# GNN and expert layer, one core: the routing of the FFN done in two halves, x and result rows by GpSimd's queue

## The chip, the cores and the metric

The kernel runs on one core of a Trainium2 chip. The metric is the device time of one execution in microseconds (us). Engines: PE is TensorE (matmuls; PEld its weight loads), DVE is VectorE, ACT is ScalarE, POOL is GpSimd, SP is SyncE, which here only issues DMAs. Each engine works through its own queue in order; an instruction that waits holds back all that is queued behind it.

## The reference, cut to what matters

There are 10,000 rows of 512 numbers, and 5,000 edges. All of it is 32-bit.

```
x = x + gnn(layernorm(x), edges)     # edge messages, two matmuls, two batch norms, silu
x = x + ffn(layernorm(x))

ffn, for each group of 16 tokens, 64 columns (16 experts x 4 sets), 32 features each:
  logits = x @ controller + tie                       # per token and column
  perm   = (logits == max of logits over the 16)      # one token for each column
  inner  = relu(the chosen token @ f1[:, column, :])  # 32 features
  result[token] = sum over columns of perm * (inner @ f2[column])
```

The change touches the FFN alone, and the last part of the GNN that runs with it: silu(scale * h2 + shift), added to x (the residual), and the layernorm of the sum.

## The kernel before, in words

The GNN ends with h2 stored in HBM by features (`h2s`). The FFN takes the 10,000 rows in ten chunks of 1024 tokens (the last has 784). A chunk has two groups `g` of 512 tokens; a group has four tiles `j` of 128; a pair `q` is two tiles, so a buffer of rows (`x2`, 512 KB) is named by `(q, g)`. The FFN of one chunk goes through these parts:

- `load_y`, `load_x`: h2 by features (four DMAs of 256 KB for each half of the chunk) and x by rows come in.
- `silu` (ACT), then `residual(j)`: PE transposes four blocks of h2 to rows in a PSUM tile `ps` (L544), DVE adds them to x (L545) and takes statistics (L546, L547). `norm(j)`: POOL works out scale and shift (L556 to L559) and writes the normalized rows `xl` (L563).
- `flip(k, q)`: PE transposes `xl` for 128 features `k` (L574), ACT copies that to `xlt` (L578). `logits`: PE multiplies by the controller (L592). `choose(q)`: DVE finds the maximum and `perm` (L608 to L611). `by_token(q)`: PE transposes `perm` (L619), DVE spreads it to `bd` (L624).
- `gather(k, g)`: PE multiplies `xl` by `bd` (L642, 32 matmuls in two PSUM tiles `pb`), so that the chosen tokens stand by column; ACT copies each tile out in two copies (L647).
- `inner(k, e)`: 64 matmuls with half of the f1 weights of features `k` (L664). After the last, ACT takes the relu (L669). Each call takes one block of weights and orders a fetch of another (`f_sb`, L477, 512 KB, five buffers).
- `outer(u, g)`: 64 matmuls with f2 (L686) into two `pb` tiles. They are copied to `it` by ACT (L696), for u of 2 and 3 one of the two by DVE (L694).
- `turn(g, u)`: DVE transposes `it` in blocks (L705). `split(q)`: POOL makes `pv` out of `perm` (L714). `scatter(q, g)`: 64 matmuls give each token its result (L735), DVE adds that to the rows (L739), and they are stored (L740).

The parts of three chunks run in one `step(a, b, e)`: chunk `b` is gathered and goes through both layers, chunk `a` after it gets its residual and its routing, and chunk `e` before it gets its results scattered. There are twelve steps; the first has only an `a`, the last only an `e`. The order of instructions on each engine is that of the calls in `step`, since nearly all are pinned (`pin` keeps the program's order).

In the order of `step` before, the gather stage holds b's gathers and inner layer with e's turns and scatters between them. All of a's residuals stand from the end of that stage into the outer stage, and all of a's flips and logits stand among b's outer calls. The logits use the PSUM tile `pi` of the inner layer. [...]

All DMAs of the FFN are issued by SP, in this order within a step: loads of a's first half of h2 and of two x buffers, the weight fetches, and, between them, each store of e followed by one load of x for a. The row buffers are 10 in turn.

## Time and profile before the change

| | us |
|---|---|
| median of 3 runs (2075.49 to 2083.97) | 2081.48 |
| the profiled execution | 2089.11 |
| its span, first to last instruction | 2087.3 |
| GNN, up to the last of its matmuls | about 1245 |
| from there to the first gather | 38.5 |
| a step of the FFN, mean of the eight from 1357.8 to 1967.0 | 76.2 |
| the last gather to the end | 120 |

The page shows one profiled execution. Busy time is given for each engine, and in the row of slices a digit is a fortieth of the span: PEclk is the clock that TensorE was granted, in tenths of full speed. A group of instructions is named by line, engine and tile (`pb<-f_sb,ib` writes pb and reads f_sb and ib). What stands in brackets or behind an arrow is what ended the wait. "issue" means that the engine waited for nothing that the profile shows.

### The profile page before, as it was taken

Reading aid. Unit: us, or ns where it says so; the run is one execution under the profiler, and the core shown is the slowest. Engines: PE = TensorE matmul, PEld = TensorE weight load, DVE = VectorE, ACT = ScalarE, POOL = GpSimd, SP = SyncE. Lnnn points to the kernel's source line nnn. Section 1 sums busy time; section 2 is a strip of 40 time slices with the busy share of each in tenths; the row PEclk is TensorE's granted clock in tenths of the full one; section 3 lists DMA queues with packets and bytes.
Section 4 is the critical chain, followed back from the end, with each engine's and each line's share of the span. In section 5 each row is a group of like instructions: output and inputs, shape, how many; then the busy total and the mean of one; then the engine's idle time right before and its main releaser. Section 6 shows DMA issues by size and latency. Waiting matters only on the chain. (4 is left out here: it accounts for less than half of the span.)

```text
span 2087.3 us, 44115 instructions
## 1 busy us (share of the span) xinstructions
PE 1821.4 (87%) x19122; PEld 998.7 (48%) x19122; DVE 1152.6 (55%) x1838; ACT 751.2 (36%) x1161; POOL 650.2 (31%) x710
## 2 busy tenths in 40 slices
PE   4885499999999989999999988888888888888765
PEld 2332244444444434444444435566566557556452
DVE  5743367777777673343344433365645645645645
ACT  1332233333333343222223113556555555455331
POOL 7144433333333233223332302412421431431410
PEclk8897699999999999999999995899889997898875
DMA  9977443444444112323233114455665564574331
GB/s 353 360 170 89 112 181 157 159 166 165 162 157 158 59 79 118 138 118 138 118 140 161 57 73 176 163 194 186 211 217 188 174 236 141 187 243 162 112 119 62
DMA packets 125720, 331.89 MB, mean 159 GB/s; under 512 B 10183, under 2 KB 10773, under 8 KB 125462
## 3 DMA queue, kind: packets, MB, share of 16 engines
q1 hardware_dynamic: 116566, 308.09, 40.5%
q0 software_dynamic: 8960, 20.98, 5.0%
q8 instruction: 151, 2.47, 0.5%
q14 instruction: 43, 0.35, 0.1%
HBM read 218.97 MB, written 110.07 MB: 158 GB/s over the span
## 5 line engine op out<-in xcount | busy, mean ns | idle before, releaser
L134 PE MATMUL x<-h_s,w_u 128*128 128x500 f32 x640 | 288.8, 584 | 0.9 <-ACT s L139 0.6
L647 ACT COPY gs<-pb 128x512 f32<-128x512 f32 x304 | 165.3, 631 | 138.9 <-PE pb L642 113.7
L642 PE MATMUL pb<-bd,xl 32*128 32x128 f32 x2504 | 183.2, 334 | 32.7 <-ACT gs L647 24.2
L134 PEld LDWEIGHTS x<-h_s,w_u 128*128 128x128 f32 x640 | 121.9, 191 | 149.3 <-issue 142.9
L696 ACT COPY it<-pb 128x1024 f32<-128x1024 f32 x120 | 120.8, 1044 | 192.4 <-PE pb L686 192.4
L642 PEld LDWEIGHTS pb<-bd,xl 32*128 32x128 f32 x2504 | 163.1, 231 | 50.2 <-ACT gs L647 28.3
L705 DVE STREAM_TRANSPOSE it<-it 128x1024 f32<-128x1024 f32 x160 | 182.4, 1207 | 0.0
L686 PE MATMUL pb<-f_sb,ib 32*32 32x256 f32 x5120 | 153.1, 411 | 27.6 <-ACT it L696 18.4
L556 POOL TENSOR_SCALAR ln_rs<-ln_mv 128x2 f32<-128x2 f32 (+2 forms) x41 | 9.1, 222 | 485.7 <-DVE ln_mv L547 472.1
L134 PE MATMUL z<-h_s,w 128*128 128x500 f32 x320 | 148.5, 587 | 3.3 <-POOL h_s L124 3.3
L144 DVE SCALAR_TENSOR_TENSOR t<-w,s 128x500 f32<-128x500 f32 x60 | 40.7, 678 | 189.3 <-PE w L134 185.9
L134 PE MATMUL z<-h_s,w_u 128*128 128x500 f32 x320 | 143.9, 582 | 0.0
L739 DVE TENSOR_TENSOR x<-pb,x 128x1024 f32<-128x1024 f32 (+1 forms) x40 | 48.1, 1204 | 159.3 <-PE pb L735 159.3
L664 PE MATMUL pi<-gs,f_sb 128*32 128x64 f32 x5120 | 110.6, 248 | 25.1 <-issue 15.9
L714 POOL TENSOR_TENSOR pv<-perm,odd_t 64x512 f32<-64x512 f32 x80 | 102.5, 1281 | 67.5 <-issue 62.5
L124 POOL TENSOR_TENSOR h_s<-hc 128x500 f32<-128x500 f32 x60 | 76.6, 1311 | 148.6 <-PE z L134 148.6
L686 PEld LDWEIGHTS pb<-f_sb,ib 32*32 32x32 f32 x5120 | 72.8, 106 | 94.0 <-ACT it L696 46.7
L735 PE MATMUL pb<-it,pv 64*32 64x256 f32 x2504 | 96.7, 435 | 22.8 <-DVE it L705 14.5
L664 PEld LDWEIGHTS pi<-gs,f_sb 128*32 128x32 f32 x5120 | 94.3, 128 | 41.7 <-issue 24.4
L139 ACT COPY s<-z 128x500 f32<-128x500 f32 x60 | 34.6, 576 | 219.4 <-PE z L134 150.8
L694 DVE COPY it<-pb 128x1024 f32<-128x1024 f32 x40 | 48.9, 1223 | 113.9 <-PE pb L686 113.3
L342 ACT ACTIVATE xt<-xt,ln_sh,ln_rs 125x512 f32<-125x512 f32 x80 | 59.6, 805 | 109.4 <-POOL ln_sh L337 109.4
(176 smaller groups left out, 3119.3 us busy)
## 6 DMA issues: line engine op xcount, KB each, us to landing
f_sb<-in_L_ffn_f_dram SPq DMA_DIRECT2D x160, 512.0 KB
h1s<-h SPq DMA_DIRECT2D x36, 1000.0 KB
agg<-zero SPq DMA_DIRECT2D x10, 2048.0 KB
xt<-in_x_dram SPq DMA_DIRECT2D x20, 1000.0 KB
at<-agg SPq DMA_DIRECT2D x20, 1000.0 KB
hc<-h1s SPq DMA_DIRECT2D x20, 1000.0 KB
h2s<-h SPq DMA_DIRECT2D x20, 1000.0 KB
x<-in_x_dram SPq DMA_DIRECT2D x39, 512.0 KB
```

Source lines behind the costliest of these rows:

```text
L124: eng.tensor_tensor(t[:, k0:k1], q(*x0, k0, k1), q(*x1, k0, k1), op)
L134: nc.tensor.matmul(bank, lhsT=us[n][:, k, m * P:(m + 1) * P], rhs=bs[n][k], start=start and k == 0, stop=k == kb - 1, skip_group_check=True)
L342: nc.scalar.activation(r, r, AF.Identity, bias=self.sh[:RT, j, :], scale=self.rs[:RT, j, :])
L642: pin(nc.tensor.matmul(pg[i][:, r % 2, j], lhsT=self.xl[g, j][s, k * P:(k + 1) * P], rhs=self.bd[s, g, j], start=True, stop=True))
L647: pin(nc.scalar.copy(to[:, 8 * i:8 * i + 8], pg[i][:, :, :, 32 * e:32 * e + 32, :].rearrange("d r j e v -> d (r j) e v")))
L664: pin(nc.tensor.matmul(self.pi[32 * q:32 * q + 32, m, :], lhsT=w[:, F * j:F * (j + 1)], rhs=gs[e][:, c, :], start=(k == 0 and m % 8 == 0), ...
L686: pin(nc.tensor.matmul(po[q // 2][o:o + 32, q % 2, t, :], lhsT=self.ib[s, 8 * e + 2 * u + t, 32 * g:32 * g + 32], rhs=self.w[e][s, t, HD * ...
L694: pin(nc.vector.tensor_copy(dst, src))
L696: pin(nc.scalar.copy(dst, src))
L705: pin(nc.vector.transpose(it, it))
L714: pin(nc.gpsimd.tensor_tensor(pv[dh * ES:(dh + 1) * ES, :, g].rearrange("c v (i t) -> c v i t", t=2 * T), self.perm[s, q].rearrange("c (i ...
L735: pin(nc.tensor.matmul(pr[32 * r:32 * r + 32, dh, i, :], lhsT=pv[s, v, g, tok], rhs=self.it[s, g, :, 2 * (4 * r + 2 * q + i) + v, :], star ...
```

## The change: what it does

- `load_y` and `silu` go by pairs `q` instead of groups `g`: half `q` of both groups in one tile, so that the first half serves tiles 0 and 1 of both groups. The first half of the next chunk is loaded in the outer stage, and its silu is done at the very end of the step before. Pieces of a DMA are 1 KB instead of 2 KB.
- `residual(j, g)` is called for one group at a time. Tiles 0 and 1 are done between the gathers; the flips and logits of the first half stand between the last gathers and inner calls; tiles 2 and 3 follow at the end of the gather stage, with `choose(0)`. Among the outer calls there remain `by_token(0)`, the flips and logits of the second half, `choose(1)` and `by_token(1)`.
- `ps` has one bank instead of two; the bank that this frees holds the logits (`pl`).
- The turns of e are dealt out in smaller lots among the gathers; `split(1)` is made later.
- x comes in by POOL's queue (but for the first chunk), and the results leave by it. Row buffers come from a list of free ones: `scatter` puts its own back, and `load_x` takes the one that has been free the longest.

```diff
-    ps_s = ctx.enter_context(tc.tile_pool(name="ps_s", bufs=2, space=PSUM))
+    ps_s = ctx.enter_context(tc.tile_pool(name="ps_s", bufs=1, space=PSUM))
+    ps_l = ctx.enter_context(tc.tile_pool(name="ps_l", bufs=1, space=PSUM))
...
+    slots = list(range(10))
...
-                n = (4 * self.c + 2 * g + q) % 10
-                x2 = self.x2[q, g] = pf.tile([P, 2, H], F32, name="x2", bufs=8) if n > 1 else pre_x[n]
+                n = self.slot[q, g] = slots.pop(0)
+                x2 = self.x2[q, g] = pf.tile([P, 2, H], F32, name=f"x2_{n}") if n > 1 else pre_x[n]
...
-                nc.sync.dma_start(out=x2[:real, :k, :], in_=self.rows(x, g, o, real, k))
+                to, src = x2[:real, :k, :], self.rows(x, g, o, real, k)
+                if self.c:
+                    pin(nc.gpsimd.dma_start(out=to, in_=src))
+                else:
+                    nc.sync.dma_start(out=to, in_=src)
...
-                pi = ps_i.tile([P, MF, G], F32, name="pi")
-                self.pl = pi.rearrange("p (q m) g -> p q (m g)", q=2)
+                self.pl = ps_l.tile([P, 2, QC], F32, name="pl")
...
-            nc.sync.dma_start(out=self.rows(out, g, o, real, k), in_=self.x2[q, g][:real, :k, :])
+            pin(nc.gpsimd.dma_start(out=self.rows(out, g, o, real, k), in_=self.x2[q, g][:real, :k, :]))
+            slots.append(self.slot[q, g])
```

The order of a step afterwards (`put` calls a part if there is such a chunk; `late` is a, but for the first chunk; `nxt` is the chunk after a; `fl` is flip, `lo` logits):

```
put(e, split, 0); gat(0, 0); turns(0, 0, 2); gat(0, 1)
put(a, residual, 0, 0); turns(0, 2, 4); gat(1, 0)
put(a, residual, 0, 1); put(a, norm, 0); inn(0, 0); turns(0, 4, 5); gat(1, 1)
put(a, residual, 1, 0); inn(0, 1); gat(2, 0)
put(a, residual, 1, 1); put(a, norm, 1); inn(1, 0); turns(0, 5, 8)
put(e, split, 1); gat(2, 1); inn(1, 1); turns(1, 0, 4); gat(3, 0)
fl(0, 0); inn(2, 0); put(late, load_y, 1)
put(e, scatter, 0, 0); put(late, load_x, 1, 0); turns(1, 4, 8); gat(3, 1)
fl(1, 0); lo(0, 0); inn(2, 1); put(a, silu, 1)
put(e, scatter, 1, 0); put(late, load_x, 1, 1); inn(3, 0)
fl(2, 0); lo(1, 0); inn(3, 1); fl(3, 0); lo(2, 0)
put(e, scatter, 0, 1); lo(3, 0)
put(a, residual, 2, 0); put(a, residual, 2, 1); put(a, norm, 2)
put(e, scatter, 1, 1)
put(a, residual, 3, 0); put(a, residual, 3, 1); put(a, norm, 3); put(a, choose, 0)
put(b, outer, 0, 0); put(nxt, load_x, 0, 0); put(nxt, load_x, 0, 1); put(nxt, load_y, 0)
put(b, outer, 0, 1); put(a, by_token, 0); put(b, outer, 1, 0); put(b, outer, 1, 1)
fl(0, 1); put(b, outer, 2, 0); fl(1, 1); lo(0, 1); put(b, outer, 2, 1)
fl(2, 1); lo(1, 1); put(b, outer, 3, 0); fl(3, 1); lo(2, 1); lo(3, 1)
put(a, choose, 1); put(b, outer, 3, 1); put(a, by_token, 1); put(nxt, silu, 0)
```

More of the change, by code (lines that the diff above doesn't have):

```diff
@@ L492, in __init__ @@
             self.tiles = [[(o, min(P, -(-(n - o) // 32) * 32), min(P, n - o)) for o in range(0, n, P)] for n in self.ns]
-            self.x2, self.st, self.mv, self.rs, self.sh, self.yt, self.xl = {}, {}, {}, {}, {}, {}, {}
+            self.x2, self.slot, self.st, self.mv, self.yt, self.xl, self.pv = {}, {}, {}, {}, {}, {}, {}
         def there(self, j):
@@ L504, in row_tile, with load_y @@
             return self.x2[j // 2, g][:, j % 2, :]
-        def load_y(self, g):
-            n = self.ns[g]
-            if g:
+        def load_y(self, q):
+            if q:
                 gs = pf.tile([P, ES // 2, G], F32, name="gs", bufs=4).rearrange("p c g -> p (c g)")
             for k in range(KH):
-                yt = gs[:, k * HC:(k + 1) * HC] if g else pre_y[k]
-                nc.sync.dma_start(out=yt[:, :n], in_=h2s[:, k, self.t0 + g * HC:self.t0 + g * HC + n])
-                if n < HC:
-                    pin(nc.vector.memset(yt[:, n:-(-n // 32) * 32], 0.0))
-                self.yt[g, k] = yt
+                yt = (gs[:, k * HC:(k + 1) * HC] if q else pre_y[k]).rearrange("p (g n) -> p g n", g=2)
+                src = h2s[:, k, self.t0:self.t0 + self.n]
+                if self.full:
+                    nc.sync.dma_start(out=yt, in_=src.rearrange("p (g q n) -> q p g n", g=2, q=2)[q])
+                else:
+                    for g in range(2):
+                        n = min(self.ns[g] - q * QC, QC)
+                        if n > 0:
+                            o = g * HC + q * QC
+                            nc.sync.dma_start(out=yt[:, g, :n], in_=src[:, o:o + n])
+                            if n % 32:
+                                pin(nc.vector.memset(yt[:, g, n:-(-n // 32) * 32], 0.0))
+                self.yt[q, k] = yt
         def rows(self, hbm, g, o, real, k):
@@ L524, in load_x, with silu, residual @@
                 o, m, real, k = self.pair(q, g)
-                n = (4 * self.c + 2 * g + q) % 10
-                x2 = self.x2[q, g] = pf.tile([P, 2, H], F32, name="x2", bufs=8) if n > 1 else pre_x[n]
+                n = self.slot[q, g] = slots.pop(0)
+                x2 = self.x2[q, g] = pf.tile([P, 2, H], F32, name=f"x2_{n}") if n > 1 else pre_x[n]
                 if real < m:
                     pin(nc.vector.memset(x2[:m, 0, :], 0.0))
-                nc.sync.dma_start(out=x2[:real, :k, :], in_=self.rows(x, g, o, real, k))
-        def silu(self, g):
-            for k in range(KH):
-                y = self.yt[g, k][:, :self.ns[g]]
-                pin(nc.scalar.activation(y, y, AF.Silu, bias=sh2[:, k:k + 1], scale=sc2[:, k:k + 1]))
-        def residual(self, j):
-            self.st[j] = pf.tile([P, 2, 6], F32, name="ln_st", bufs=2)
-            self.mv[j] = pf.tile([P, 2, 2], F32, name="ln_mv", bufs=2)
-            for g in self.there(j):
-                o, m, _ = self.tiles[g][j]
+                to, src = x2[:real, :k, :], self.rows(x, g, o, real, k)
+                if self.c:
+                    pin(nc.gpsimd.dma_start(out=to, in_=src))
+                else:
+                    nc.sync.dma_start(out=to, in_=src)
+        def silu(self, q):
+            for k in range(KH):
+                yt = self.yt[q, k]
+                ns = [min(n - q * QC, QC) for n in self.ns]
+                for y in [yt] if ns == [QC, QC] else [yt[:, g, :n] for g, n in enumerate(ns) if n > 0]:
+                    pin(nc.scalar.activation(y, y, AF.Silu, bias=sh2[:, k:k + 1], scale=sc2[:, k:k + 1]))
+        def residual(self, j, g):
+            if g == 0:
+                self.st[j] = pf.tile([P, 2, 6], F32, name="ln_st", bufs=2)
+                self.mv[j] = pf.tile([P, 2, 2], F32, name="ln_mv", bufs=2)
+            if g in self.there(j):
+                _, m, _ = self.tiles[g][j]
                 x2 = self.row_tile(g, j)[:m, :]
@@ L543, in residual @@
                 for k in range(KH):
-                    pin(nc.tensor.transpose(py[:m, k * P:(k + 1) * P], self.yt[g, k][:, o:o + m], ident))
+                    o = (j % 2) * P
+                    pin(nc.tensor.transpose(py[:m, k * P:(k + 1) * P], self.yt[j // 2, k][:, g, o:o + m], ident))
                 pin(nc.vector.tensor_add(x2, py[:m, :], x2))
@@ L719, in split @@
                         ALU.mult))
-            return pv
+            self.pv[q] = pv
         def scatter(self, q, g):
@@ L739, in scatter, with step, put @@
             pin(nc.vector.tensor_add(x2, pr[:real, :, :k, :].rearrange("p h j d -> p j h d"), x2))
-            nc.sync.dma_start(out=self.rows(out, g, o, real, k), in_=self.x2[q, g][:real, :k, :])
-    def step(a, b, e):
-        gs = {}
+            pin(nc.gpsimd.dma_start(out=self.rows(out, g, o, real, k), in_=self.x2[q, g][:real, :k, :]))
+            slots.append(self.slot[q, g])
+    def step(a, b, e, nxt):
+        gs, xs = {}, {}
+        def put(c, f, *args):
+            if c:
+                f(c, *args)
         def gat(k, g):
@@ L755, in turns @@
         def turns(g, u0, u1):
-            if e:
-                for u in range(u0, u1):
-                    e.turn(g, u)
-        def back(q, g):
-            if e:
-                e.scatter(q, g)
-        def load(*which):
-            if a and a.c > 0:
-                for q, g in which:
-                    a.load_x(q, g)
-        def res(j):
-            if a:
-                a.residual(j)
-                a.norm(j)
-        def out_of(u, g):
-            if b:
-                b.outer(u, g)
-        xs = {}
+            for u in range(u0, u1):
+                put(e, Chunk.turn, g, u)
         def fl(k, q):
@@ L786, in lo @@
                 a.logits(k, q, *xs.pop((k, q)))
-        if e:
-            e.pv = [e.split(q) for q in range(2)]
+        late = a if a and a.c > 0 else None
+        put(e, Chunk.split, 0)
         gat(0, 0)
-        if a and a.c > 0:
-            a.load_y(0)
-        load((0, 0), (1, 0))
+        turns(0, 0, 2)
         gat(0, 1)
-        turns(0, 0, 8)
+        put(a, Chunk.residual, 0, 0)
+        turns(0, 2, 4)
         gat(1, 0)
+        put(a, Chunk.residual, 0, 1)
+        put(a, Chunk.norm, 0)
@@ L797, in step @@
         inn(0, 0)
+        turns(0, 4, 5)
         gat(1, 1)
+        put(a, Chunk.residual, 1, 0)
         inn(0, 1)
         gat(2, 0)
+        put(a, Chunk.residual, 1, 1)
+        put(a, Chunk.norm, 1)
         inn(1, 0)
-        turns(1, 0, 4)
+        turns(0, 5, 8)
+        put(e, Chunk.split, 1)
         gat(2, 1)
         inn(1, 1)
-        back(0, 0)
-        load((0, 1))
+        turns(1, 0, 4)
+        gat(3, 0)
+        fl(0, 0)
+        inn(2, 0)
+        put(late, Chunk.load_y, 1)
@@ L807, in step @@
+        put(e, Chunk.scatter, 0, 0)
+        put(late, Chunk.load_x, 1, 0)
         turns(1, 4, 8)
-        gat(3, 0)
-        inn(2, 0)
         gat(3, 1)
-        inn(2, 1)
-        if a:
-            if a.c > 0:
-                a.load_y(1)
-            a.silu(0)
-        back(1, 0)
-        load((1, 1))
-        inn(3, 0)
-        inn(3, 1)
-        if a:
-            a.silu(1)
-        back(0, 1)
-        res(0)
-        back(1, 1)
-        res(1)
-        out_of(0, 0)
-        res(2)
-        out_of(0, 1)
@@ L829, in step @@
-        res(3)
-        out_of(1, 0)
-        fl(0, 0)
-        out_of(1, 1)
         fl(1, 0)
         lo(0, 0)
+        inn(2, 1)
+        put(a, Chunk.silu, 1)
+        put(e, Chunk.scatter, 1, 0)
+        put(late, Chunk.load_x, 1, 1)
+        inn(3, 0)
         fl(2, 0)
         lo(1, 0)
-        out_of(2, 0)
+        inn(3, 1)
         fl(3, 0)
         lo(2, 0)
+        put(e, Chunk.scatter, 0, 1)
         lo(3, 0)
-        if a:
-            a.choose(0)
-        out_of(2, 1)
+        put(a, Chunk.residual, 2, 0)
@@ new lines, in step @@
+        put(a, Chunk.residual, 2, 1)
+        put(a, Chunk.norm, 2)
+        put(e, Chunk.scatter, 1, 1)
+        put(a, Chunk.residual, 3, 0)
+        put(a, Chunk.residual, 3, 1)
+        put(a, Chunk.norm, 3)
+        put(a, Chunk.choose, 0)
+        put(b, Chunk.outer, 0, 0)
+        put(nxt, Chunk.load_x, 0, 0)
+        put(nxt, Chunk.load_x, 0, 1)
+        put(nxt, Chunk.load_y, 0)
+        put(b, Chunk.outer, 0, 1)
+        put(a, Chunk.by_token, 0)
+        put(b, Chunk.outer, 1, 0)
+        put(b, Chunk.outer, 1, 1)
@@ L844, in step @@
         fl(0, 1)
-        if a:
-            a.by_token(0)
+        put(b, Chunk.outer, 2, 0)
         fl(1, 1)
         lo(0, 1)
-        out_of(3, 0)
+        put(b, Chunk.outer, 2, 1)
         fl(2, 1)
         lo(1, 1)
+        put(b, Chunk.outer, 3, 0)
         fl(3, 1)
@@ L854, in step @@
         lo(3, 1)
-        if a:
-            a.choose(1)
-        out_of(3, 1)
-        if a:
-            a.by_token(1)
+        put(a, Chunk.choose, 1)
+        put(b, Chunk.outer, 3, 1)
+        put(a, Chunk.by_token, 1)
+        put(nxt, Chunk.silu, 0)
     chunks = [Chunk(c) for c in range(NC)]
     at = lambda c: chunks[c] if 0 <= c < NC else None
-    for g in range(2):
-        chunks[0].load_y(g)
-    for g in range(2):
-        for q in range(2):
+    for q in range(2):
+        for g in range(2):
             chunks[0].load_x(q, g)
+        chunks[0].load_y(q)
+    chunks[0].silu(0)
     for _ in range(5):
@@ L870, in gnn_ffn_kernel @@
     for c in range(-1, NC + 1):
-        step(at(c + 1), at(c), at(c - 1))
+        step(at(c + 1), at(c), at(c - 1), at(c + 2))
 def _constants():
```

## The prediction

> **What bounds the kernel now.** I began with the page's first two parts. They say that TensorE (PE) is the busiest engine, and that its clock is not always whole.

> ```profile
> span 2087.3 us, 44115 instructions
> PE 1821.4 (87%) x19122; PEld 998.7 (48%) x19122; DVE 1152.6 (55%) x1838; ACT 751.2 (36%) x1161; POOL 650.2 (31%) x710
> PEclk8897699999999999999999995899889997898875
> ```

> The first 1,245 us (the GNN) are untouched. The FFN starts there; a step of it begins where the gather matmuls (L642) follow the outer ones (L686): 1283.3, 1357.8, 1430.4, 1503.3, 1580.2, 1659.1, 1734.4, 1814.4, 1890.9, 1967.0. The eight steps from 1357.8 to 1967.0 take 76.2 us each. I cut three of them at the first outer matmul, into a gather stage and an outer stage; the last row below is the bare outer layer of the last step.

> ```profile
> core 0: us, PE busy (x) PEld busy (x) DVE busy (x) ACT busy (x) POOL busy (x), PEclk, DMA share, GB/s
> 1430.40:1471.80 41.40, 35.41 (x1040) 28.87 (x1040) 25.58 (x29) 24.48 (x42) 0.00 (x0) 0.96 0.63 207
> 1471.80:1503.30 31.50, 26.75 (x597) 13.93 (x596) 18.79 (x31) 16.18 (x20) 21.83 (x32) 1.00 0.56 202
> 1734.40:1782.70 48.30, 44.79 (x1042) 37.21 (x1044) 25.31 (x28) 24.31 (x42) 0.00 (x0) 0.72 0.55 186
> 1782.70:1814.40 31.70, 26.67 (x597) 13.90 (x596) 18.99 (x32) 16.18 (x20) 21.84 (x32) 1.00 0.54 187
> 2031.80:2055.00 23.20, 16.55 (x380) 6.98 (x348) 3.54 (x3) 8.84 (x9) 2.53 (x2) 0.50 0.19 70
> ```

> So with a whole clock a step is 41.4 + 31.5 = 72.9 us, of which PE is idle 6.0 + 4.8; the rest of the 76.2 is half clock in the gather stage (48.3 us at 0.72). Then I asked what ended waits in the eight steps, SyncE's queue (SP) too.

> ```profile
> SPq L529 <- DMA out_dram<-x: 116.8, 30, 6.3
> ...
> PE pi L664 <- issue: 14.9, 9, 3.3
> ...
> PE pb L735 <- issue: 8.1, 6, 3.2
> ...
> PE pi L664 <- ACT ib L669: 5.9, 7, 1.1
> ```

> The reader sees that each load of x waits in the queue until the store just before it has landed, and that PE lacks instructions or weights ("issue") 24 us in eight steps, 3.0 a step. The queue in order of time gives what one such pair takes:

> ```profile
> 1459.96 0.44 SPq L740 DMA_DIRECT2D out_dram<-x  x1
> 1460.50 1.31 SPq L477 DMA_DIRECT2D f_sb<-in_L_ffn_f_dram  x2
> 1468.17 0.37 SPq L529 DMA_DIRECT2D x<-in_x_dram  x1
> 1468.64 1.13 SPq L740 DMA_DIRECT2D out_dram<-x  x1
> 1474.92 0.37 SPq L529 DMA_DIRECT2D x<-in_x_dram  x1
> ```

> From store to load is 8.2 and 6.3 us here; over all 30 pairs it is 2.9 to 8.2, median 5.3. Today this costs PE little: the x so loaded is wanted only at the later residuals.

> **Costs on PE, start to start in the order of time at whole clock.** One gather call 1.65 us (1453.19 to 1454.84), an inner call 1.03, a scatter 1.90, four transposes of a residual 0.51, a flip 0.58, a pair of logits 0.58, an outer call 1.42. On DVE: residual add, statistics and aggregate 0.70 + 0.72 + 0.20, scatter's add 1.22, a turn 1.14. On ACT: one silu 0.74, a copy of L696 1.0.

> **What moves into the gather stage.** Residuals of tiles 0 and 1 were there already; tiles 2 and 3 (four calls), four flips and four logits come in: 4 x 0.51 + 4 x 0.58 + 4 x 0.58 = 6.7 us. Gains: the wait for the relu before the last inner call is filled (0.9, as at 1459.92 with 0.77); SP's queue no longer holds fetches behind x, of whose 3.0 us I count half, 1.5[...] (bounds 0 and 3.0). The silu of the next chunk's first half now stands on ACT between the last outer copy and the first gather copy. Before, ACT idled 1.29 us there (1503.27 to 1504.56); four silus take 3.0, so the gathers' copies come 1.7 later and PE waits 1.5 of it, having two buffers of pb.

> **The x loads on GpSimd's queue (POOL).** The free list is empty when scatter(0,0) gives its slot back, and load (1,0) takes that very slot; likewise load (1,1) takes that of scatter(1,0). So POOL issues: out(0,0), wait, x(1,0), out(1,0), wait, x(1,1), out(0,1), norm 2, out(1,1), norm 3. What is new is that tile x(1,1) is wanted in the same stage, by the residual (tile 2, g=1). From the end of scatter(1,0) on PE, as zero: add done at 1.3; store issued at 1.4; load issued 5.3 later, and 0.5 more because POOL's issue is longer, at 7.2; issued at 8.2, landed 4.9 later (the 5.3 without SP's issue of 0.4), 13.1. No plain DMA of POOL is in the trace: an issue costs between 0.95 us (the row of L229, 949 ns for 128 rows of 2 KB) and twice that (256 rows here). I take 1.0, the row.

> PE meanwhile has inner, flip, logits, inner, flip, logits, scatter, logits, residual, residual, scatter: 9.8 us, about 1 more for the second residual, which waits for the first one's add since ps has one bank. The next residual (tile 3, g=0) needs that bank too: x at 13.1, add to 13.8, so PE stands from 10.8 to 13.8. DVE then does statistics (14.7), scatter's add (15.9), the next add (16.6); the fourth residual starts at 16.7, the outer layer at 17.2. Without stalls it would be 10.8: 6.4 us lost a step. Norm 3, behind all that on POOL, ends near 22 and is wanted by flip(0,1) after four outer calls, near 31: hidden, with 9 us of slack.

> [...] Gather stage: +6.7 - 0.9 - 1.5 + 1.5 + 6.4 = +12.2 us.

> **The outer stage** loses the same 6.7 us of PE work, but the work was cover. An outer call fills both buffers of pb at its end; with nothing between, the next waits for two ACT copies:

> ```profile
> 2034.70 3.25 PE L686 MATMUL pb<-f_sb,ib 32*32 32x256 f32 x64 [1.12 <-ACT it L696]
> 2039.03 3.26 PE L686 MATMUL pb<-f_sb,ib 32*32 32x256 f32 x64 [1.07 <-ACT it L696]
> ```

> That is 4.35 us a call at half clock; at whole clock 2.0 of copies, 0.2 of signals and 1.27 of matmuls, 3.45. Four such calls (u = 0, 1; only by_token between) are 13.8; the four with a flip or logits beside them about 3.0 each, 12; the ends 1.2: 27.0, so -4.5.

> [...] The stage starts with a whole or a half clock; I take 1.0 a step.

> Sum for a middle step: +12.2 - 4.5 + 1.0 = +8.7. Eight steps have both stores and late loads: +70.

> **Once only.** Start: 1244.8 to 1283.3 now. With one ps bank each residual goes PE 1.1 (half clock), DVE 0.7, signals, 1.9 us, and flips wait for norm 1, then silu stands between flips 1 and 2 on ACT. Laid out from 1252.1: 7.6 + norm 4.8 + flips and silu 10.1 + residuals 7.6 + norm 4.8 + flips 6.5 + choice 3.2, that is 1296.7; less some overlap, +11 (bounds 0 and +14).

> Last chunk: DVE's memsets of gs (8 x 1.76 us) stand behind up to eight turns, and PE waits:

> ```profile
> 1986.61 2.20 PE L642 MATMUL pb<-bd,xl 32*128 32x128 f32 x18 [5.75 <-ACT gs L647]
> ...
> 2011.26 2.21 PE L642 MATMUL pb<-bd,xl 32*128 32x128 f32 x18 [7.25 <-ACT gs L647]
> ```

> With the turns dealt out 2, 2, 1, 3, 4, the memsets come earlier: -8 of these 13.

> At no cost: y loads by halves (1 MB as before, ordered some 9 us ahead of their silu; late, they would hold silu and the flips' copies); residuals amid the gathers (a gather or inner call lies between two, so one bank suffices; DVE's two turns ahead of each add are 2.3 us); logits' own bank (three gathers lie before the first inner call, nothing waits for pi today); split in halves (5.1 us each on a POOL idle in that stage; the second stands ahead of POOL's first store and is wanted at scatter(1,0), 7 us later; if POOL ran late there, that scatter would wait). Last stores by POOL: +1.

> Sum: +70 + 11 - 8 + 1 = +74. The profiled execution was 2089.1 us (span 2087.3), 7.6 above the median 2081.5; so 2163 on its scale and 2155 on the median's. I forecast 2154.

> **Rivals.**
> [...]
> [...]
> Clock worse: half clock through all outer stages, 3.6 in place of 1.0, and about 1.3 more for the flips, logits and calls of its second half: +3.9 a step, 31 in all, 2185. For it: the bare outer layer above; against: the outer stages of today, 1.00.
> The move of x and stores does nothing and the re-ordering cancels: 2081, within 0.5%.

> **Chances.** Mine 0.52, short landing 0.16, clock worse 0.12, faster 0.13, nothing 0.07. Mine alone reaches from 2125 (start at no cost, -11, and landing 1 us shorter, which counts twice a step, -16) to 2180 (store's issue at 1.9 and start at +14). The range for 8 in 10 takes in short landing and nothing below, and most of the worse clock above: 2078 to 2190; outside lie the faster case and an end of the worse one. Faster by over 0.5% 0.13, within 0.5% (about what measuring this kernel can tell from no change) 0.08, slower 0.79.

> **What would show it.** POOL: a wait of 4 us or more before the load lines, on out_dram<-x. DVE: the residual's add of tile 2, g=1 waiting for DMA x. PE: waits on that add ahead of the outer layer, 5 to 7 us a step; gather stage near 53 us, outer stage near 27 at whole clock; 13 us to the first gather more at the start. A gather stage under 46 us, or an x landed before the second residual's transposes end, makes me wrong.

## The result, and the profile after

The changed kernel takes 2192.53 us (median of 4 runs, 2188.19 to 2197.57) beside 2082.72 for the kernel before: a ratio of 1.053, 95% interval 1.0487 to 1.0573. It is slower, as forecast, but by 110 us where the forecast had 73, and it ends 2.5 us above the range. Its profiled execution took 2189.3 us. The page, its first lines:

```profile
span 2187.1 us, 44096 instructions
PE 1862.3 (85%) x19122; PEld 1006.2 (46%) x19122; DVE 1148.5 (53%) x1838; ACT 748.8 (34%) x1165; POOL 705.5 (32%) x786
PEclk9967799999999999999999966888898878787985
```

PE is busy for 41 us more than before with the same 19122 matmuls, and the row of its clock has gone from nines with a few eights to eights and sevens: in the FFN, the right two fifths of the row, a middle step now has 29.0 of its 87.7 us at half clock, before 13.7 of 76.2. Steps begin at 1292.0, 1372.7, 1459.1, 1547.5, 1633.2, 1718.9, 1809.9, 1902.0, 1990.5 and 2074.0. Two of them, cut at the first outer matmul as before (start and end, length, busy time by engine, granted clock, DMA share, GB/s):

```profile
core 0: us, PE busy (x) PEld busy (x) DVE busy (x) ACT busy (x) POOL busy (x), PEclk, DMA share, GB/s
1372.70:1431.70 59.00, 48.00 (x1088) 36.44 (x1088) 34.16 (x43) 26.14 (x46) 16.34 (x26) 0.86 0.51 171
1431.70:1459.10 27.40, 22.10 (x551) 10.63 (x550) 9.73 (x17) 13.90 (x17) 11.29 (x15) 0.88 0.50 176
1809.90:1870.90 61.00, 48.64 (x1088) 36.66 (x1088) 34.49 (x44) 26.16 (x46) 16.74 (x27) 0.84 0.50 165
1870.90:1902.00 31.10, 27.13 (x551) 12.29 (x550) 9.59 (x16) 14.04 (x17) 10.88 (x14) 0.65 0.44 155
```

The gather stage is 57 to 61 us in the eight middle steps (forecast 53), and the outer stage depends on its clock: 27.4 at 0.88, 31.1 at 0.65. What ended the waits in the eight steps from 1372 to 2074 (sum in us, times, longest):

```profile
POOL xl L581 <- issue: 76.1, 8, 10.0
POOL x L541 <- DMA out_dram<-x: 68.1, 14, 7.4
PE ps L562 <- DVE x L563: 38.9, 22, 4.3
PE ps L592 <- POOL xl L581: 26.4, 15, 3.0
DVE x L563 <- DMA x<-in_x_dram: 22.9, 8, 5.2
PE pb L659 <- ACT gs L664: 16.5, 8, 2.1
```

Three waits of PE are large now: 38.9 for the residual's add (the late x, and the one bank), 26.4 for POOL's normalized rows, 16.5 for a gather's copy behind the silus. They are 10.2 us a step. The third was there before, smaller:

```profile
PE pb L642 <- ACT gs L647: 6.9, 14, 0.7
```

"issue", 3.0 a step before, is 5.7 us in eight steps. One step shows each wait in its place, first PE (the second row is gather (3, 0)):

```profile
1462.87 3.11 PE L659 MATMUL pb<-bd,xl 32*128 32x128 f32 x32 [2.06 <-ACT gs L664]
...
1482.11 1.95 PE L659 MATMUL pb<-bd,xl 32*128 32x128 f32 x32
...
1487.71 1.23 PE L592 MATMUL ps<-ident,xl 128*128 128x128 f32 x3 [2.99 <-POOL xl L581]
...
1509.35 0.65 PE L562 MATMUL ps<-ident,gs 128*128 128x128 f32 x4 [0.82 <-DVE x L563]
...
1516.22 0.66 PE L562 MATMUL ps<-ident,gs 128*128 128x128 f32 x4 [4.32 <-DVE x L563]
1518.87 1.11 PE L562 MATMUL ps<-ident,gs 128*128 128x128 f32 x4 [1.99 <-DVE x L563]
```

and what POOL did meanwhile:

```profile
1483.57 1.52 POOL L581 TENSOR_SCALAR xl<-x,ln_rs,ln_sh 128x512 f32<-128x512 f32 x2 [9.00 <-issue]
...
1502.26 0.73 POOL L757 DMA_DIRECT2D out_dram<-x  x1 [1.12 <-DVE x L756]
1509.43 0.73 POOL L541 DMA_DIRECT2D x<-in_x_dram  x1 [6.44 <-issue]
```

The second row is the store of scatter (1, 0); the load of the third takes its buffer, 7.2 us later (between them POOL stands 6.44), and DVE's add for tile 2, g=1, which waits for that load, runs at 1515.47. (Of the 16 late loads of these steps the profile puts 14 down to the store's landing; this one it gives as "issue".) PE's 4.32 is this delay, the longest of the eight steps (2.1 in the mean); of the 1.99 behind it only a part is, since 1.4 are left where x comes in time (e1). The 9.00 us ahead of norm 0's rows are another wait, which the prediction doesn't have: `xl` has eight buffers (L581's tile) and a chunk has eight tiles, so the first rows of the next chunk go into a buffer that this chunk's gathers still read. The profile calls the wait "issue" and so does not name the reader, but in each of the eight steps the write begins 0.3 to 0.4 us after the 16th of the 32 matmuls of the stage's seventh gather, (3, 0), the last that reads tiles of group 0. No run gave `xl` more buffers. POOL's second pair follows only at 1486.89, and the flip right behind that gather wants it.

### The profile page after: what moved, and what is told of

It reads as the page before. It is cut to its first block, busy times and chain, and to the rows that moved or that the text cites. A ratio compares the mean times of both kernels' runs of the same rounds, so it can differ in the third digit from the quotient of the medians.

```text
span 2187.1 us, 44096 instructions
## 1 busy us (share of the span) xinstructions
PE 1862.3 (85%) x19122; PEld 1006.2 (46%) x19122; DVE 1148.5 (53%) x1838; ACT 748.8 (34%) x1165; POOL 705.5 (32%) x786
## 5 line engine op out<-in xcount | busy, mean ns | idle before, releaser
L664 ACT COPY gs<-pb 128x512 f32<-128x512 f32 x304 | 163.4, 622 | 156.7 <-PE pb L659 139.3
L703 PE MATMUL pb<-f_sb,ib 32*32 32x256 f32 x5120 | 179.9, 481 | 42.2 <-ACT it L713 40.5
L659 PE MATMUL pb<-bd,xl 32*128 32x128 f32 x2504 | 176.0, 326 | 31.6 <-ACT gs L664 22.0
L659 PEld LDWEIGHTS pb<-bd,xl 32*128 32x128 f32 x2504 | 156.1, 224 | 50.9 <-ACT gs L664 27.3
L703 PEld LDWEIGHTS pb<-f_sb,ib 32*32 32x32 f32 x5120 | 81.3, 116 | 129.3 <-ACT it L713 97.1
L563 DVE TENSOR_TENSOR x<-ps,x 128x512 f32<-128x512 f32 x79 | 54.3, 687 | 144.2 <-PE ps L562 120.2
```

Of the source, the lines that this page charges most:

```text
L563: pin(nc.vector.tensor_add(x2, py[:m, :], x2))
L659: pin(nc.tensor.matmul(pg[i][:, r % 2, j], lhsT=self.xl[g, j][s, k * P:(k + 1) * P], rhs=self.bd[s, g, j], start=True, stop=True))
L664: pin(nc.scalar.copy(to[:, 8 * i:8 * i + 8], pg[i][:, :, :, 32 * e:32 * e + 32, :].rearrange("d r j e v -> d (r j) e v")))
L703: pin(nc.tensor.matmul(po[q // 2][o:o + 32, q % 2, t, :], lhsT=self.ib[s, 8 * e + 2 * u + t, 32 * g:32 * g + 32], rhs=self.w[e][s, t, HD * ...
```

## The experiments

Ratios are to the kernel before, with 95% intervals; "us" behind a ratio is its difference to 1.053, or to 1 for edits of the kernel before, times 2083 us. Busy, idle and half-clock times of a stage are means over the eight middle steps of the trace.

**Parts of the new order undone.** e1 stores another buffer's rows at scatter (1, 0), so that load x(1, 1) waits for no landing (these rows of the output are not the result):

```diff
-            pin(nc.gpsimd.dma_start(out=self.rows(out, g, o, real, k), in_=self.x2[q, g][:real, :k, :]))
+            own = self.x2[q, g] if (q, g) != (1, 0) or self.c == NC - 1 else chunks[self.c + 1].x2[1, 0]
+            pin(nc.gpsimd.dma_start(out=self.rows(out, g, o, real, k), in_=own[:real, :k, :]))
```

> The changed kernel, but the store of pair (1,0) sends the rows of the next chunk's buffer (same size, same queue) in place of its own, so that output is left wrong; the load of x (1,1) then waits for DVE's add alone and not for a landing. Theory X (the late x is the main loss, as the prediction had it): 5 to 6 us a step in eight steps, 40 to 48 us faster than the changed kernel. Theory L (POOL's norms wait for the buffers of xl, which the gathers read until gat(3,0), and the flip waits for them; half clock follows): x costs only what the trace shows as waits on it, 22.5 us in seven steps, so 20 to 28 us faster, and about 80 us remain above the kernel before.

Measured: 1.0304 (1.0261 to 1.0347), -47 us. One of its steps, gather stage and outer stage:

```profile
1615.60:1671.90 56.30, 47.15 (x1095) 35.54 (x1098) 34.23 (x43) 26.02 (x46) 16.68 (x26) 0.85 0.53 179
1671.90:1697.70 25.80, 19.92 (x551) 10.00 (x550) 9.70 (x18) 13.95 (x17) 10.97 (x15) 1.00 0.52 187
```

The outer stage has its whole clock back: half clock there goes from 10.5 us a step to none. Of the 4.9 us that a step gains, 1.0 is idle time of PE and 3.9 is busy time. So what the late x costs here is for the larger part busy time in the work behind it, at half clock. PE's waits for the residual's add fall from 38.9 us to 17.5 in the eight steps: those that are left, 2.2 us a step, come without a late x, at the second and the fourth residual of tiles 2 and 3, which follow another one with no gather or inner call between.

e2 makes the flip that waits for POOL's rows two parts later:

```diff
         gat(3, 0)
-        fl(0, 0)
         inn(2, 0)
...
         gat(3, 1)
+        fl(0, 0)
+        inn(2, 1)
         fl(1, 0)
         lo(0, 0)
-        inn(2, 1)
```

> The changed kernel, but flip(0,0) stands behind gat(3,1), and flip(1,0) with the first logits behind inn(2,1); nothing else moves. Theory L: PE waited 3.3 us a step for xl ahead of flip(0,0), and the inner and scatter calls behind it ran at half clock (about 2 us more), so 26 to 45 us faster than the changed kernel. Theory X alone: the wait shifts to the late x, since its chain on POOL starts with the scatter's add, less than 15 us faster.

Measured: 1.0424 (1.0371 to 1.0478), -22 us, between its two theories. The wait for `xl`, 26.4 us, is gone from PE's large ones, but part of it comes back elsewhere: in the eight steps PE waits 46.6 us for the residual's add (38.9 without this edit) and 16.5 for "issue" (5.7). A step of the trace is 2.9 us shorter, of which 0.7 is idle time of PE and 2.2 busy time; half clock falls from 29.0 us a step to 23.5.

e3 puts the residuals of tiles 2 and 3 back among the outer calls:

```diff
-        put(a, Chunk.residual, 2, 0)
-        put(a, Chunk.residual, 2, 1)
-        put(a, Chunk.norm, 2)
         put(e, Chunk.scatter, 1, 1)
-        put(a, Chunk.residual, 3, 0)
-        put(a, Chunk.residual, 3, 1)
-        put(a, Chunk.norm, 3)
         put(a, Chunk.choose, 0)
         put(b, Chunk.outer, 0, 0)
+        put(a, Chunk.residual, 2, 0)
+        put(b, Chunk.outer, 0, 1)
+        put(a, Chunk.residual, 2, 1)
+        put(a, Chunk.norm, 2)
+        put(b, Chunk.outer, 1, 0)
+        put(a, Chunk.residual, 3, 0)
+        put(b, Chunk.outer, 1, 1)
...
```

> The changed kernel, but the residuals of tiles 2 and 3 go back among the outer calls, one between each two of the first four; the flips and logits of the second half follow from u = 2 on. The x that is late is then wanted some 8 us later, and the bare outer calls have cover and a whole clock. Theory X with bare calls: 5 to 7 us a step from the waits, 1 to 3 from the outer stage, 45 to 75 us faster than the changed kernel. Theory L: 25 to 40 us faster, since the wait for xl stays.

Measured: 1.0221 (1.0172 to 1.0271), -64 us. The gather stage is 52.0 us, the outer stage 30.3: the residuals are cover there again, and x may come late.

**Parts put into the kernel before.** e4 is the queue alone: x and the results by GpSimd, buffers by turns.

> The kernel before with one part of the change alone: x (but for the first chunk) and result rows by POOL's queue, pinned. If that part is harmful by itself: norms queued behind a store's landing hold the residuals' rows and the flips, 3 to 6 us a step, 2110 to 2140 us. If the queue is only harmful where x is wanted in the same stage: within 10 us of the kernel before; a gain of up to 24 us if the waits for 'issue' came from SP's queue.

Measured: 1.0015 (0.9984 to 1.0047), no difference. POOL waits for the stores there as well (60.2 us in 13 waits between 1372 and 1890 us); what hangs on those loads is wanted a stage later. In these steps SP's queue holds no load of x and no store, yet PE's waits for "issue" are still there (25.0 us in the gather stages of eight steps, 23.0 before). The larger part is that of the inner calls (window 1366 to 1940 us):

```profile
PE pi L668 <- issue: 20.6, 9, 4.5
```

e5 is the banks alone:

```diff
-    ps_s = ctx.enter_context(tc.tile_pool(name="ps_s", bufs=2, space=PSUM))
+    ps_s = ctx.enter_context(tc.tile_pool(name="ps_s", bufs=1, space=PSUM))
+    ps_l = ctx.enter_context(tc.tile_pool(name="ps_l", bufs=1, space=PSUM))
...
-                self.pl = pi.rearrange("p (q m) g -> p q (m g)", q=2)
+                self.pl = ps_l.tile([P, 2, QC], F32, name="pl")
```

> The kernel before with one part alone: one bank of ps, the other bank for the logits. There two residuals stand back to back, so that the second waits for DVE's add: 0.8 us for four of eight residuals and about 0.7 for each flip that follows another user of ps, 3 to 6 us a step, 25 to 50 us slower than the kernel before. If ps is not what costs: within 10 us of it.

Measured: 1.0283 (1.0225 to 1.0341), +59 us. PE's largest wait in 7 of its steps:

```profile
PE ps L545 <- DVE x L546: 29.6, 28, 1.5
```

28 residuals wait about 1 us each for the add of the one ahead, 4.2 us a step, which is 34 of the 59 us in eight steps. In this order residuals stand back to back.

**Combinations.** e6 is e2 with e3, e7 is e6 with the next chunk's four silus dealt out among the last outer calls (as in the diff of e17), e8 is e1 with e2.

> The changed kernel with the orders of two earlier runs together: residuals of tiles 2 and 3 among the outer calls, flip(0,0) behind gat(3,1). If the late x and the wait for xl are two losses that add: 64 + 22, near 86 us faster than the changed kernel, within 1.5% of the kernel before. If the second only moves the wait: no better than the residuals' order alone (about 2134 us).

> The run before this one, and the silu of the next chunk's first half is dealt out, one of four activations behind each of the last four outer calls in place of all four ahead of the gathers. Theory: PE's wait of 2 us ahead of gat(0,1) goes back to 0.7 us and with it the half clock that begins 3 us into each step and lasts 10 us, 2 to 5 us a step, 16 to 45 us faster than the run before. If the clock falls there anyway (as it does in the kernel before): 8 to 12 us.

> The changed kernel with the store of pair (1,0) sent from another buffer (its output is left wrong) and flip(0,0) behind gat(3,1). If the late x and the wait for xl add: 47 + 22, near 70 us faster than the changed kernel, about 2125 us. If the outer stage's clock was what both paid for: 50 to 55 us.

Measured: e6 1.0145 (1.0113 to 1.0176), -80 us where the single edits sum to 86; e7 1.0064 (1.0022 to 1.0107), -97; e8 1.0249 (1.0216 to 1.0282), -59 where they sum to 69. The three orders undone in e7 take back 97 of the 110 us. Two gather stages of e7:

```profile
1438.00:1477.50 39.50, 37.51 (x1072) 29.52 (x1072) 28.48 (x34) 24.34 (x43) 13.10 (x19) 1.00 0.68 212
1508.90:1558.90 50.00, 46.46 (x1074) 35.37 (x1074) 28.77 (x34) 24.17 (x43) 14.48 (x21) 0.80 0.57 182
```

The calls are the same; one had the whole clock and took 10.5 us less. What decides this was the next question.

**The clock.** e9 adds two useless pairs of matmuls a step to e7; e10 adds the same two to the kernel before:

```diff
+        def warm(self):
+            for g in range(2):
+                pin(nc.tensor.matmul(self.pl[g * ES:(g + 1) * ES, 1, :QC], lhsT=ctl[:, 0, :], rhs=self.perm[:, 1, :],
+                                     start=True, stop=True, skip_group_check=True))
...
         gat(0, 0)
+        put(b, Chunk.warm)
...
         put(a, Chunk.by_token, 1)
+        put(a, Chunk.warm)
```

> The kernel of e7 (residuals of tiles 2 and 3 back among the outer calls, flips one call later, silu dealt out; 1.0064 of the kernel before) plus two useless pairs of matmuls of the logits' kind (0.6 us each, results overwritten), one after by_token(1), one behind the first gather. Theory (the clock is halved because the array does little in the first gathers): they fill PE's waits there, the gather stages keep the whole clock, a step goes from about 80 us to 72 to 75, eight steps give 40 to 60 us: about 2040, ratio 0.975 to 0.985. Rival (the clock falls at a set place whatever PE does there): a step costs 1.2 us more, ratio 1.009 to 1.013.

> The kernel before plus the same two useless pairs of matmuls a step, one after by_token(1), one behind the first gather. Theory of the fill: the gather stage, half clock for some 7 us a step now, keeps the whole clock: 3 to 4 us a step less, 1.2 more for the fill itself if nothing hides it: ratio 0.985 to 0.995. Rival: the clock falls anyway, ratio 1.003 to 1.007.

e11 deals the turns out in the kernel before; e12 is e10 with e11:

```diff
-        turns(0, 0, 8)
+        turns(0, 0, 4)
...
+        turns(0, 4, 5)
...
-        turns(1, 0, 4)
+        turns(0, 5, 8)
...
+        turns(1, 0, 4)
+        gat(3, 0)
+        inn(2, 0)
...
-        gat(3, 0)
-        inn(2, 0)
```

> The kernel before with only the turns of the chunk before dealt out in five lots (4, 1, 3, 4, 4) among the gathers, the first scatter after inner call (2, 0). The prediction's term for the last chunk: its memsets on DVE no longer stand behind eight turns, so -8 us once, nothing in the other steps: ratio 0.996. Rival: the later turns hold the first scatter in every step, about 1 us each: ratio 1.000 to 1.004.

> The kernel before with both of these edits. If they are independent, the ratio is the product of the two single ones: 0.981 to 0.991 by the theory of the fill, 1.000 to 1.008 by its rival.

Measured: e9 0.9953 (0.9925 to 0.998), half of what its theory wanted, e10 0.9868 (0.9817 to 0.9918), e11 0.9968 (0.9943 to 0.9994), e12 0.984 (0.9796 to 0.9884), near the product of e10 and e11, 0.9836. Work that computes nothing makes the kernel before and that of e7 faster. The first 20 us of a step of the kernel before, and then of e12:

```profile
1734.40:1754.40 20.00, 19.31 (x354) 17.89 (x354) 14.28 (x15) 10.98 (x20) 0.00 (x0) 0.60 0.32 105
```
```profile
1713.10:1733.10 20.00, 19.64 (x584) 17.50 (x592) 14.31 (x15) 15.12 (x28) 0.00 (x0) 1.00 0.47 158
```

PE counts as busy for the same time; at 0.60 it records 354 matmuls, at 1.00 it records 584. In the eight steps half clock in the gather stage falls from 13.2 us a step to 1.7, and PE's busy time from 39.3 to 36.0 although one of the two pairs, 0.65 us, came into that stage (the other stands at the end of the outer stage): 4.0 us for 11.5, or 0.34 us for each us of half clock. In e10, where the turns are not dealt out, 9.0 us of half clock a step are left: the fills alone keep the first gathers whole in five of the eight steps. e12 is 33 us faster than the kernel before and 144 faster than the changed one.

The changed kernel with the same two pairs is e13; with three more (behind the second gather, ahead of the flip that waits, ahead of the first outer call) it is e14; e14 with the store of e1 is e16. e15 is e5 with the two pairs.

> The changed kernel plus the two useless pairs of matmuls of e10, one after by_token(1), one behind the first gather. Theory: a part of the +110 us is clock that falls in the first gathers; filled, it stays whole there, and a step gains 4 to 6 us of the 11: ratio 1.03 to 1.038. Rival: the waits for xl and x make the clock fall by themselves later in the step, so that the fill brings less than it costs: 1.050 to 1.058.

> The changed kernel with five such pairs a step: also behind the second gather, ahead of the flip that waits for POOL's xl, and ahead of the first outer call. Theory: what stays with a whole clock is the waits alone, and they are 3.3 (xl) and 5.2 (x) us a step, some 70 us in all of the 110: ratio 1.022 to 1.032. Rival: the fills themselves (3 us a step, none of it hidden) take back what they bring: 1.035 to 1.05.

> The kernel of e5 (the kernel before, ps with one bank, logits with their own; 1.0283) plus the two pairs of e10. Theory: one bank costs by waits of PE on DVE, which the fill leaves: 1.012 to 1.020. Rival: one bank costs by the clock that these waits bring down: filled, as e10, 0.987 to 0.997.

> e14 with the store of e1 (scatter (1, 0) stores a buffer of the next chunk, so its rows in the output are not the result, and no load waits for it). It takes the wait for x away from a kernel whose clock is filled. Theory: what x costs by its wait alone is 5 us a step, 40 us in all: e14's ratio less 0.019. Rival: most of what e1 brought (47 us) was clock: e14's ratio less 0.01 or less.

Measured: e13 1.045 (1.0377 to 1.0522), -17 us, not clear of the changed kernel's interval and between theory and rival; e14 1.067 (1.059 to 1.075); e15 1.0081 (1.0055 to 1.0107); e16 1.0635 (1.0564 to 1.0706). Against e10, e15 gives the bank's price with the same fills in both: 0.0213, or 44 us; the ratio itself lies between the two expectations. (Their clocks are not equal: in the gather stage half clock is 9.0 us a step in e10's trace, 4.3 in e15's.) Most of it is waits: the row shown of e5 reads 30.1 us in seven steps here, 34 in eight. e14 cannot tell what it was made for: the fill ahead of the outer layer writes the bank that DVE still reads for `choose`, and PE waits 12.4 us for that in six steps. e16 has PE's waits for the residual's add down from 30.1 to 13.0 us in six steps, 2.9 a step, but its step is only 1.1 shorter, and the 7 us by the medians are within the intervals. Half clock is 32.0 us a step in both, more than the 29.0 of the changed kernel: the clock was not filled, so that e16 could not set the wait apart from the clock as it was meant to.

Why e13 brought so little stands in its trace, where a middle step is 87.8 us, as without the fills: half clock is 1.9 us less in the gather stage and 4.4 more in the outer stage. PE at the start of a step:

```profile
1453.70 0.65 PE L634 MATMUL pl<-perm,ctl 128*64 128x256 f32 x4
1454.43 1.72 PE L666 MATMUL pb<-bd,xl 32*128 32x128 f32 x32
1456.08 0.65 PE L634 MATMUL pl<-perm,ctl 128*64 128x256 f32 x4
1458.21 3.05 PE L666 MATMUL pb<-bd,xl 32*128 32x128 f32 x32 [1.47 <-ACT gs L671]
```

The fills (L634) run, and a wait of 1.47 us is left behind them, for a copy that stands on ACT behind four silus; the next gather call runs at half clock, 3.05 us where a whole one takes 1.72. e17 deals the silus out in the changed kernel, and e18 is e17 with the two pairs:

```diff
         put(b, Chunk.outer, 2, 1)
+        put(nxt, Chunk.silu, 0, (0,))
...
         put(b, Chunk.outer, 3, 0)
+        put(nxt, Chunk.silu, 0, (1,))
...
         lo(3, 1)
+        put(nxt, Chunk.silu, 0, (2,))
...
-        put(nxt, Chunk.silu, 0)
+        put(nxt, Chunk.silu, 0, (3,))
```

> The changed kernel with the four silus of the next chunk's first half dealt out on ACT, one each behind outer calls (2, 1) and (3, 0), the last logits, and the step's end, in place of all four at the end. The prediction's term: PE waits 1.5 us a step less for the gathers' copies, 12 us in eight steps: ratio about 1.047. If the half clock of the first gathers goes with that wait, 4 us a step more: 1.030 to 1.035. Rival: the clock falls there all the same: 1.047 or above.

> e17 plus the two useless pairs of matmuls of e13. Theory: e13's fill brought little because one wait of 1.5 us for a gather's copy stood where the fill didn't reach, behind the silus on ACT; with that gone, the first gathers keep the whole clock in nearly every step, some 5 us a step less than the changed kernel: ratio 1.030 to 1.036. Rival: the clock falls for another cause: no lower than e17 by more than 0.003, or above it.

Measured: e17 1.0339 (1.0305 to 1.0373), -40 us; e18 1.024 (1.0205 to 1.0275), -60 us. Half clock in the first 20 us of a step is 10.2 us in every one of the eight steps of the changed kernel, in four of e17, in none of e18. The same start of a step in e18:

```profile
1451.39 0.65 PE L634 MATMUL pl<-perm,ctl 128*64 128x256 f32 x4
1452.12 1.72 PE L666 MATMUL pb<-bd,xl 32*128 32x128 f32 x32
1453.77 0.65 PE L634 MATMUL pl<-perm,ctl 128*64 128x256 f32 x4
1454.54 2.15 PE L666 MATMUL pb<-bd,xl 32*128 32x128 f32 x32
```

So the half clock of the first gathers goes in half of the steps with the wait behind the silus alone, and in all with the two pairs as well. The wait is 2.1 us a step in the changed kernel where it was 0.9 before, 1.2 more, put at 1.5. In e17 it is 0.7 again; for these 1.4 us a step of the trace is 3.3 shorter (1.0 of it idle time of PE, 2.3 busy time), and 5.1 in e18. The medians' 40 and 60 us would be 5.0 and 7.5 a step if all of them lay in the eight steps.

## Why the prediction was right in direction and wrong in size

The profiled spans differ by 99.8 us. Set against the sum of the prediction, in us a middle step (stages' means; the clock in the gather stage is the rise of half clock from 13.2 to 18.5 us at the 0.34 of e12, an estimate; in the outer stage it is the mean of 28.3 less the mean of 26.1 that the same calls take with a whole clock in e1):

| step of the prediction | forecast | measured |
|---|---|---|
| moved work, gather stage | +6.7 | +6.9 (busy +8.7 less the clock) |
| relu's wait and "issue" | -2.4 | -2.9 (waits 3.6 to 0.7) |
| silu ahead of the gathers' copies | +1.5 | +1.2 (0.9 to 2.1) |
| late x, one bank | +6.4 | +4.9 |
| waits for POOL's `xl` | not seen | +3.3 |
| half clock, gather stage | 0 | +1.8 |
| outer stage at whole clock | -4.5 | -5.9 |
| half clock, outer stage | +1.0 | +2.3 |
| sum | +8.7 | +11.5 (87.7 less 76.2; the terms round to 11.6) |

The table says where the time went, not what each wait would give back: in e1, e2 and e17 most of the gain is busy time.

Eight steps make +92 where I had +70. The first gather starts 8.7 us later (forecast 11), the end comes 7.3 sooner after the last step's start (forecast -8 and +1), and step 0, which the sum left out, is 6.2 longer: 92.2 + 8.7 + 6.2 - 7.3 = 99.8. The other 10 us to the medians' 110 lie around the profiles: that of before stood 6.4 above the median of 2082.72, that of after 3.2 below its own, and its execution was 0.4 longer outside the span.

**Right.** That the late x, the lost cover and the start would cost more than the relu's wait, "issue" and the memsets give back was the forecast, and each of these shows. The chain of the late x is as laid out: in the step shown the load is issued 8.8 us after the end of scatter (1, 0) on PE (forecast 7.2), and the add of tile 2, g=1 begins at 14.9 (13.1). PE stood 7.1 us in that step (0.82, 4.32 and 1.99), but that is the most in any of the eight; the mean is 4.9, against 6.4. A DMA's issue took POOL 0.73 us (1.0). A short landing, for which I had 0.16, did not come. The page's row of POOL's stores (count, size, median time from issue to landing) has 4.6, beside the 4.9 of the forecast:

```profile
out_dram<-x POOLq DMA_DIRECT2D x39, 512.0 KB, 4.6
```

The start is within 2.3 us. That the move of the queue alone costs nothing is shown by e4, in the order of before.

"One bank suffices" was said of the residuals amid the gathers, and it held: in the eight steps none of these 32 residuals waits for it. The wait of the second late residual, put at about 1 us, is 1.05 in the mean. What e5 measures, +59 us, is the price of one bank in the old order. In the new one e1 leaves 2.2 us a step of waits for the add without a late x; what the clock makes of these stays open, since the changed order with two banks for `ps` was not tried. In the last chunk PE waits 3.92 and 1.43 us for the copies behind the memsets where it waited 5.75 and 7.25, 7.7 less of the 8 forecast:

```profile
2080.37 2.24 PE L659 MATMUL pb<-bd,xl 32*128 32x128 f32 x18 [3.92 <-ACT gs L664]
...
2089.13 1.69 PE L659 MATMUL pb<-bd,xl 32*128 32x128 f32 x18 [1.43 <-ACT gs L664]
```

Alone, this dealing out measured -7 us (e11); in that trace it is 14 less behind the last step's start and 1.4 more in a middle step. Half clock there is 1.7 us more in the gather stage, so that a part of the 1.4 is the clock; the rest, one trace does not tell from chance.

**Right by luck.** The outer stage (-3.6 for -3.5) is two errors that cancel: 1.4 too little gained at whole clock and 1.3 too little lost to half clock. And "issue" fell, but not for the reason given. The 1.5 for it in the sum was a choice, half of the 3.0 of the trace; no run shows that half, nor whether the waits are for weights or for instructions (the page of before has a DMA queue for instructions, 151 packets, and ties it to no wait); in the changed kernel they come to 0.7 us a step. e4 takes x off SP's queue as well and keeps it, and in e2, where a large wait of PE is gone, 16.5 us of it are back. That PE no longer came early enough to meet these waits fits both; it is not shown.

**Wrong.** Two steps failed. First, the routing half was looked at for what POOL issues after scatter (0, 0), not for what norm 0 and norm 1 wait for: by the trace the buffers of `xl` come free only with gather (3, 0), and the flip stands right behind it. These waits, 26.4 us in eight steps or 3.3 a step, were not in the sum; e2, without them, is 22 us faster. Second, the clock was put at 1.0 us a step ("I take 1.0 a step") and only in the outer stage; it is 4.1, in both stages. No run shows the 1.0, which was my choice: the outer stages came to 2.3 and the gather stages to 1.8, where I had none. What failed is that each new wait was priced at its own length: in e17 1.4 us of wait less made a step 3.3 shorter, and in e1 four fifths of the gain was busy time, with half clock in the outer stage down from 10.5 us a step to none. The two steps make 6.4 us a step more than the sum had; that the sum is only 2.8 short is due to the late x (1.5 less), the outer stage at whole clock (1.4) and smaller terms.

The upper end of the prediction's own case, 2180, does not come out of its terms either: an issue at 1.9 us counts 0.9 twice a step, 14 us in eight, and the start 3, which makes about 2171.

The rival "clock worse" put its 31 us in the outer stages alone (its 3.6 is four times the 0.9 between the 4.35 and the 3.45 of a bare call, an estimate); nearly half of the loss to the clock was in the gathers, where no case had more half clock than before. "Faster", for which I had 0.13, did not come. Work in the gaps went with less half clock in the gather stage in e10 (9.0 us a step) and e12 (1.7) than before (13.2), but in the changed kernel (18.5) the silus made a gap that nothing filled.

## What to carry to other kernels

Price a new wait on TensorE with what it adds to the busy time of the work behind it, not with its length alone: here 1.4 us of it taken away (e17) made a step 3.3 us shorter. Before moving the producer of a buffer ahead, count the buffers and find who still reads the oldest, and ask of a shared slot which load will take it next and when that is wanted. Where work on a starving stretch is cheap, fill the gap: two useless pairs of matmuls a step took 27 us off the kernel before.
